# Decoder layer: five shared score banks, one pool for weights and transposed weights, block transposes in every duo

## Chip, cores and metric

The kernel runs on one core of a Trainium2 chip. The metric is device time in microseconds (us). Beside the runs that give the time there is one profiled execution; all lines of a profile come from it.

## The reference

One decoder layer on x of shape (4 batches, 1024 rows, 256 columns), all in float32. Three blocks follow one another, each on a layer norm of x and each added to x:

```
x = x + attn(layernorm(x))        # 16 heads of 64, 4 key/value heads, softmax over 1024 keys
x = x + cross_attn(layernorm(x))  # 16 heads of 16, 64 context rows
x = x + ffn(layernorm(x))         # routes each row to one of 64 tiles, gathers that tile's spline and direction
```

The first block is most of the work: for each batch and head `scores = q @ k.T` (1024 x 1024), `probs = softmax(scores)`, `out = probs @ v`.

## The kernel before

**Tiles and steps.** The queries of a batch are cut into 8 query tiles of 128 rows. A query tile has 16 heads. They are taken two at a time, and such a pair is a step: head z=0 lies on partitions 0 to 63 and head z=1 on partitions 64 to 127 of the query and key tiles. Two steps make a duo (`duo`, L566), four duos a query tile. In all there are 4 x 8 x 4 = 128 duos and 256 steps.

**One step.** TensorE writes the scores of two heads, 128 queries x 1024 keys each, into two PSUM tiles `s` of two banks each (`scores`, L589 to L598: four matmuls of 128x512, key half by key half). VectorE finds each row's maximum (`largest`, L606). ScalarE takes the exponential from PSUM into the SBUF tile `prob` and sums the rows on the way (`exponential`, L612). There are two such `s` tiles in the pool, so a step fills the pool, and the next step's matmuls write into the tiles that the exponentials are reading.

**Transposing.** The product with the values needs the weights with the keys on the partitions. Three of four duos (`by_array` false, L453) get there in two moves: VectorE transposes every 32x32 block in place (`turn`, L621, one instruction for a head), and then SyncE issues 16 DMAs of 128 KB (`carry`, L648) that carry blocks of 32 partitions from `prob` to their place in `probT`. Each fourth duo goes through TensorE: 32 transposes by the identity into the small PSUM tiles (`flips`, L631) and 8 ScalarE copies of 128x512 into `probT` (`evict`, L635).

**Values and output.** `values` (L671) multiplies `probT` with the values into the PSUM tile `av`, which has a bank of its own (`ps_o`), and ScalarE copies it to `heads` (L686). Once per query tile (`project`, L691) the row sums are inverted, turned (`rsT`), written to DRAM and spread back over the partitions (`rb`, L717 and L707, on SyncE's queue), GpSimd divides (`divide`, L710), and TensorE projects (`out_rows`, L728).

**PSUM.** Two `s` tiles of two banks, one bank for `av`, and three banks `p1` which every other matmul shares (`psum1`, L241): eight banks.

**What sets the order.** The order on every queue is planned while the program is built. Each piece of work is a `Task` with an engine, an assumed cost in us and a key (its due step). `Flow.order` (L120) plays the queues: it picks the task that could start first, urgent ones (scores, maxima, exponentials) ahead on a tie, and it holds a task that isn't urgent back if an urgent one will be ready within that task's cost (`soon`, L140 and L153). Tiles come in a number of places by tag (L228); a `Task` that takes a tile waits for a free place. The real tile pool hands its buffers out in turn. Each engine then executes its queue in the order that was written.

Of the kernel before, what the change touches and what calls it, by code (L numbers as in the profile page):

```python
# [17 lines left out]
P = 128  # L18
# [38 lines left out]
class Buf:  # L57


    def __init__(self, tag=None, make=None, whole=None):  # L60
        self.tag, self.make, self.whole = tag, make, whole or self
        self.writers, self.readers, self.parts = [], [], {}
        self.uses, self.first, self.left, self.last, self.t = set(), None, 0, 0.0, None

# [13 lines left out]
class Flow:  # L78
# [7 lines left out]
    AHEAD, SLACK = 16, 0.4  # L86
    LAG = {"PE": 0.3, "DVE": 0.2, "ACT": 0.25, "POOL": 0.25}
# [5 lines left out]
    def add(self, engine, cost, key, emit, reads=(), writes=(), lag=None, holds=(), lead=False, urgent=False):  # L93
# [4 lines left out]
        for b in writes:  # L98
            t.need.update(b.readers)
        t.need.discard(t)  # L100
# [19 lines left out]
    def order(self):  # L120
        free = {tag: [0.0] * n for tag, n in self.places.items()}
# [14 lines left out]
        while todo:  # L136
            best = None
            for engine, some in could.items():
                pick = None
                soon = min((t.ready for t in some if t.urgent), default=inf)  # L140
                for t in some:
# [4 lines left out]
                    for b in t.takes:  # L146
# [4 lines left out]
                        start = max(start, free[b.tag][k])  # L151
                    else:
                        if not t.urgent and start < soon < start + t.cost - self.SLACK:  # L153
                            start = soon
# [10 lines left out]
            for b in t.takes:  # L165
                free[b.tag].pop(0)
                if b.tag in self.lines:
                    self.lines[b.tag].remove(b)
# [8 lines left out]
            for b in t.bufs:  # L177
                b.left -= 1
                b.last = max(b.last, t.end)
                if not b.left:  # L180
                    insort(free[b.tag], b.last + 0.2)
            yield t

    def emit(self):
        for t in self.order():
            for b in t.takes:
                b.t = b.make()
# [5 lines left out]
def decoder(  # L193
# [26 lines left out]
    ps_s = ctx.enter_context(tc.tile_pool(name="ps_s", bufs=2, space=PSUM))  # L220
    ps_1 = ctx.enter_context(tc.tile_pool(name="ps_1", bufs=3, space=PSUM))
    ps_o = ctx.enter_context(tc.tile_pool(name="ps_o", bufs=1, space=PSUM))
# [5 lines left out]
            s=2, p1=3, o=1, x=3, xn1=2, xT=1, kT0=1, kT1=1, vn=4, qT=12, prob=2, probT=2, sums=3, nmax=4,  # L228
# [8 lines left out]
    def buf(tag, pool, *shape, bufs=None, name=None):  # L237
        bufs = flow.places[tag] if bufs is None else bufs
        return Buf(tag, lambda: pool.tile([P, *shape], F32, tag=tag, name=name or tag, bufs=bufs))

    def psum1(name):  # L241

        return Buf("p1", lambda: ps_1.tile([P, 512], F32, tag="p1", name=name))
# [159 lines left out]
    def layernorm(key, name, src, dst, w, reads, writes):  # L403

        st = Buf("ln", lambda: (
            small.tile([P, w, 6], F32, tag="bnst", name=f"{name}_st", bufs=2),
            small.tile([P, w, 2], F32, tag="bnmv", name=f"{name}_mv", bufs=2),
            small.tile([P, w], F32, tag="bnrs", name=f"{name}_rs", bufs=2),
# [20 lines left out]
        add("DVE", 0.6 * w, key, stats, reads, [st], holds=writes)  # L429
        add("POOL", 1.0, key, rsqrt, [st], [st])  # L430
        add("ACT", 0.45 * w, key, apply, [st, *reads], writes)

    def transposed(key, name, src, dst, k, reads, write):
# [12 lines left out]
        add("PE", 0.55, key, flips, reads, [pt], holds=[write])  # L446
# [6 lines left out]
    halves = (slice(0, HD), slice(HD, P))  # L453
    xs, xTs, kTs, vns, qTs, sums, heads = {}, {}, {}, {}, {}, {}, {}

    def by_array(d):

        return d % 4 == 3
# [27 lines left out]
    def keys(b, j, key):  # L486

        kT = kTs[b, j] = buf(f"kT{j}", big, S, name=f"kT_{b}_{j}")
        for g in range(2):
# [15 lines left out]
            add("PE", 1.75, key, project, [wk_, xTs[b].part(2 * g), xTs[b].part(2 * g + 1)], [pk], holds=[kT])  # L505
            add("ACT", 0.7, key, evict, [pk, colv_], [kT])

    def value_rows(b, g, key):
# [24 lines left out]
        add("PE", 1.75, key, project, [wv_, xTs[b].part(g)], [pv], holds=[vn])  # L533
        add("DVE", 0.69, key, evict, [pv, rowv_], [vn])

    def queries(b, w, c, key):
# [16 lines left out]
        add("PE", 1.8, key, project, [wq_, xTs[b].part(w)], [pq], holds=[qTs[b, w, c], qTs[b, w, c + 1]])  # L553
# [12 lines left out]
    def duo(b, d):  # L566
# [7 lines left out]
        prob = Buf("prob", lambda: work.tile([P, 4 * S], F32, tag="prob", name=f"prob_{b}_{d}"))  # L574
        probT = Buf("probT", lambda: work.tile([P, 4 * S], F32, tag="probT", name=f"probT_{b}_{d}"))
# [7 lines left out]
        for i in range(2):  # L583
# [3 lines left out]
            ps = [Buf("s", lambda z=z: ps_s.tile([P, S], F32, tag="s", name=f"s_{b}_{d}_{i}_{z}")) for z in range(2)]  # L587

            def scores(ps=ps, q=q, kT=kT):  # L589
                for g in range(2):  # L590
                    for z, r in enumerate(halves):
                        mm(  # L592
                            ps[z].t[:, 512 * g : 512 * (g + 1)],
# [6 lines left out]
            add("PE", 1.95, n - 3, scores, [q, kT], ps, holds=[prob, ss], lead=True)  # L600
            for z in range(2):
                k = z * QC + c
                nmax = buf("nmax", small, 1, name=f"nmax_{b}_{d}_{i}_{z}")

                def largest(z=z, nmax=nmax, ps=ps):
                    nc.vector.tensor_reduce(nmax.t, ps[z].t, AX.X, ALU.max, negate=True)  # L606

                def exponential(z=z, i=i, k=k, nmax=nmax, ps=ps):
                    src = ps[z].t
# [6 lines left out]
                add("DVE", 1.22, n - 3, largest, [ps[z]], [nmax], urgent=True)  # L616
                add("ACT", 1.33, n - 3, exponential, [ps[z], nmax], [prob.part((z, i)), ss.part(k)], urgent=True)
                if not by_array(d):
# [4 lines left out]
                    add("DVE", 1.25, n - 1, turn, [prob.part((z, i))], [prob.part((z, i))])  # L623
                else:
                    for g in range(2):
# [11 lines left out]
                        add("PE", 0.54, n - 1, flips, [prob.part((z, i))], [pt], holds=[probT])  # L637
                        add("ACT", 0.6, n - 1, evict, [pt], [probT.part((z, g))])

        if not by_array(d):  # L640


            for k in range(4):
                for qb in range(4):
                    r = (qb + k) % 4

                    def carry(qb=qb, r=r):
# [6 lines left out]
                        "SP", 0.6, at, carry, [prob.part((z, i)) for z in range(2) for i in range(2)],  # L654
# [4 lines left out]
        av = Buf("o", lambda: ps_o.tile([P, 2 * P], F32, tag="o", name=f"av_{b}_{d}"))  # L659
        jp = e // 2  # L660
        for part in range(2):
            def values(part=part):
                for kc in range(4 * part, 4 * part + 4):
                    for z, r in enumerate(halves):
# [3 lines left out]
                        else:  # L668
# [3 lines left out]
                            av.t[r, :],  # L672
# [7 lines left out]
                "PE", 1.9, at + 1, values,  # L680
# [4 lines left out]
        def evict():  # L685
            nc.scalar.copy(hd.t.rearrange("p c q -> p (c q)"), av.t)  # L686

        add("ACT", 0.45, at + 1, evict, [av], [hd])


    def project(b, qt):  # L691
# [4 lines left out]
        rT = Buf("rsT", lambda: small.tile([H, P], F32, tag="rsT", name=f"rsT_{b}_{qt}", bufs=1))  # L696
        rD = Buf("rsD", lambda: dram.tile([2, QC, P], F32, tag="rsD", name=f"rsD_{b}_{qt}"))
# [21 lines left out]
        for z, r in enumerate(halves):  # L719
            add("SP", 0.5, at - 4, lambda z=z, r=r: spread(z, r), [rD], [rb.part(z)], lag=2.5)  # L720
        for e in range(QC // 2):
            add("POOL", 0.6, at - 1, lambda e=e: divide(e), [rb.part(0), rb.part(1), hT[e]], [hT[e]])
        xb = x_part(b, qt)
        po, t = psum1(f"po_{b}_{qt}"), buf("res", work, D, name=f"res_{b}_{qt}")
        for part in range(2):
# [4 lines left out]
            add("PE", 1.75, at, out_rows, hT[2 * part : 2 * part + 2] + [wo_] + [po] * part, [po], holds=[t])  # L730
# [66 lines left out]
    def cross_attention(b, t0, at):  # L797
# [27 lines left out]
        add("PE", 1.8, at + 1, project_q, [xT, xwq_], [pq], holds=[qT])  # L825
# [3 lines left out]
        for k in range(TX):  # L829
# [15 lines left out]
            add("PE", 1.1, now, scores, [qT, kblk], ps, holds=[sc])  # L845
            for z in range(2):
# [9 lines left out]
                add("DVE", 0.75, now, masked, [ps[z], mneg_], [sc])  # L856
# [30 lines left out]
            add("POOL", 1.6, now + 1, add_up, [sc], [half], holds=[rs])  # L887
# [34 lines left out]
            add("PE", 0.9, now + 3, values, [pT.part(0), pT.part(1), vblk], [av], holds=[oT])  # L922
# [18 lines left out]
            add("PE", 0.9, now + 4, project_o, [oT, xwo_], [po], holds=[r])  # L941
# [4 lines left out]
    def calibrated(at, name, score, w, reads):  # L946
# [3 lines left out]
        def new(tag, *shape):  # L950
            return small.tile([P, *shape], F32, tag=tag, name=f"{name}_{tag}", bufs=1)
# [351 lines left out]
```

## Time and profile before

| | |
|---|---|
| median of 3 runs | 1978.22 us (1977.18 to 1980.28) |
| profiled execution | 1978.13 us, of which the span from first to last instruction is 1976.4 us |
| mean granted TensorE clock | 0.939 |
| busy in the span | TensorE 1737.7, VectorE 1400.9, ScalarE 1062.5, GpSimd 554.1 us |
| DMA | 243.05 MB; SyncE's queue takes 49.6% of 16 engines' span |
| first and last score matmul group start at | 36.8 and 1866.0 us |

Reading: the span splits into a head (36.8 us until the first scores), 255 intervals between steps (1829.2 us, 7.17 us each) and a tail (110.4 us from the start of the last scores). A line of a profile names the source line, the engine, the operation, what is written and read, the count, the busy time in us, the mean ns of one, and the idle time of the engine just before it with what ended that. A float32 matmul shows as two records.

### The profile page before, as it was taken

To read this page: it belongs to the slowest core of one execution; us is meant where nothing else is said; L and a number is where in the kernel's file an instruction comes from. 1 tells how busy PE (TensorE), PEld (TensorE's weight loads), DVE (VectorE), ACT (ScalarE), POOL (GpSimd) and SP (SyncE) were. 2 spreads that over 40 slices of the span, in tenths; PEclk is the share of its full clock that TensorE was granted. 3 is DMA by queue.
4 is the path that set the end of the run, shared out by engine and by line. 5 is a ranking of instruction groups with operands and counts; after the bars stand their busy time and mean duration, and the time that the engine had idled before them with its cause. 6 is when DMAs were issued, how large, how long until landed. Compare 5 with 4: busy or idle time off the path is not lost.

```text
span 1976.4 us, 28894 instructions
## 1 busy us (share of the span) xinstructions
PE 1737.7 (88%) x10180; PEld 1025.7 (52%) x10180; DVE 1400.9 (71%) x2036; ACT 1062.5 (54%) x1977; POOL 554.1 (28%) x872
## 2 busy tenths in 40 slices
PE   6898989889998998989999898988999899997842
PEld 4455555555654555555655454555555455554521
DVE  4667777886778766787677676787677876778632
ACT  3445556656564655655565555655565455555511
POOL 1001213152122512225031522316122350304352
PEclk8889999999998999999999898999999899999965
DMA  3566455455655455566454456545555645445500
GB/s 131 128 139 150 115 140 122 115 146 125 138 129 136 106 137 124 121 152 150 102 134 107 123 136 139 139 116 126 136 116 116 157 118 129 105 111 130 139 23 12
DMA packets 95455, 243.05 MB, mean 123 GB/s; under 512 B 28368, under 2 KB 39376, under 8 KB 95312
## 3 DMA queue, kind: packets, MB, share of 16 engines
q1 hardware_dynamic: 91504, 229.39, 49.6%
q0 software_dynamic: 2704, 9.46, 1.7%
q10 hardware_dynamic: 1104, 2.37, 0.3%
q8 instruction: 81, 1.33, 0.3%
q14 instruction: 62, 0.51, 0.1%
HBM read 35.32 MB, written 4.46 MB: 20 GB/s over the span
## 4 chain that ended last, share of the span: by engine, by line
PE 64%; DVE 16%; ACT 6%; POOL 5%; DMA 3%; SPq 3%; issue 3%; POOLq 0%; DVEq 0%; ACTq 0%
PE s L592 22%; PE av L671 18%; DVE nmax L606 6%; PE pq L545 5%; PE po L728 4%; PE ptp L631 4%; DVE prob L621 3%; SPq L648 3%; ACT prob L612 3%; PE pk L494 1%; PE pv L517 1%; DMA par<-in_table,tile 1%; PE pxt L898 1%; PE xs L837 1%; PE pxq L814 1%
## 5 line engine op out<-in xcount | busy, mean ns | idle before, releaser
L606 DVE TENSOR_REDUCE nmax<-s 128x1 f32<-128x1024 f32 x512 | 601.9, 1216 | 342.7 <-PE s L592 341.4
L612 ACT ACTIVATE prob<-s,nmax 128x1024 f32<-128x1024 f32 x512 | 568.8, 1114 | 407.3 <-DVE nmax L606 388.7
L592 PE MATMUL s<-kT,qT 64*128 64x512 f32 x2048 | 584.4, 639 | 35.0 <-ACT prob L612 34.6
L671 PE MATMUL av<-probT,vn 128*64 128x256 f32 x4096 | 499.4, 396 | 29.5 <-DMA probT<-prob 26.0
L621 DVE STREAM_TRANSPOSE prob<-prob 128x1024 f32<-128x1024 f32 x384 | 458.6, 1223 | 37.7 <-ACT prob L612 26.8
L671 PEld LDWEIGHTS av<-probT,vn 128*64 128x64 f32 x4096 | 298.2, 142 | 252.3 <-issue 111.7
L592 PEld LDWEIGHTS s<-kT,qT 64*128 64x128 f32 x2048 | 212.9, 192 | 266.5 <-issue 163.6
L710 POOL TENSOR_TENSOR heads<-heads,rb 128x256 f32<-128x256 f32 x128 | 90.0, 729 | 607.6 <-DMA rb<-rsD 503.7
L635 ACT COPY probT<-ptp 128x512 f32<-128x512 f32 x256 | 137.8, 590 | 74.3 <-PE ptp L631 72.5
L631 PE MATMUL ptp<-ident,prob 128*128 128x128 f32 x1024 | 141.1, 281 | 34.0 <-ACT prob L612 30.4
L631 PEld LDWEIGHTS ptp<-ident,prob 128*128 128x128 f32 x1024 | 112.8, 143 | 82.4 <-issue 37.6
L545 PE MATMUL pq<-ln_T,wq 128*128 128x256 f32 x512 | 127.6, 394 | 12.3 <-DVE xsc L849 12.3
L863 POOL TENSOR_TENSOR xsc<-xsc,xmx 128x1024 f32<-128x1024 f32 x32 | 61.2, 1914 | 248.2 <-DVE xmx L860 136.7
L728 PE MATMUL po<-wo,heads 128*128 128x256 f32 x512 | 119.2, 383 | 1.6 <-POOL heads L710 1.6
L545 PEld LDWEIGHTS pq<-ln_T,wq 128*128 128x128 f32 x512 | 95.3, 194 | 47.9 <-issue 29.2
L728 PEld LDWEIGHTS po<-wo,heads 128*128 128x128 f32 x512 | 95.5, 190 | 29.8 <-POOL heads L710 9.2
L612 ACT ACTIVATION_READ_ACCUMULATOR prob<-s,nmax 128x1 f32 x512 | 101.0, 197 | 0.0
L427 ACT ACTIVATE ln_n<-x,ln_mv,ln_rs 128x256 f32<-128x256 f32 x64 | 36.6, 596 | 107.1 <-POOL ln_mv L422 107.1
L686 ACT COPY heads<-av 128x256 f32<-128x256 f32 x128 | 47.6, 372 | 76.3 <-PE av L671 73.9
L556 ACT ACTIVATE qT<-pq,bqs,qscale 128x256 f32<-128x256 f32 x128 | 65.6, 564 | 35.6 <-PE pq L545 35.5
L419 POOL TENSOR_SCALAR ln_rs<-ln_mv 128x1 f32<-128x1 f32 (+1 forms) x96 | 21.4, 222 | 213.2 <-DVE ln_mv L415 200.7
L441 PE MATMUL ln_pt<-ident,ln_n 128*128 128x128 f32 x192 | 37.2, 312 | 44.9 <-ACT ln_n L427 42.4
(166 smaller groups left out, 1498.1 us busy)
## 6 DMA issues: line engine op xcount, KB each, us to landing
probT<-prob SPq DMA_DIRECT2D x1536, 128.0 KB, 2.3
rb<-rsD SPq DMA_DIRECT2D x64, 256.0 KB, 3.9
ln_n<-in_x SPq DMA_DIRECT2D x16, 256.0 KB, 3.1
x<-in_x SPq DMA_DIRECT2D x8, 512.0 KB, 4.9
out<-ln_n POOLq DMA_DIRECT2D x7, 512.0 KB, 4.9
wq<-in_w_qT ACTq DMA_DIRECT2D x1, 1024.0 KB, 8.0
wo<-in_w_oT SPq DMA_DIRECT2D x1, 1024.0 KB, 12.6
rowv<-in_rows ACTq DMA_DIRECT2D x1, 774.0 KB, 10.6
```

What stands on the lines that cost most here:

```text
L545: mm(pq.t[:, 2 * P * k : 2 * P * (k + 1)], lhsT=wq[:, dc, (c + k) * P : (c + k + 1) * P], rhs=xTs[b].t[:, dc, 2 * P * w : 2 * P * (w + 1)] ...
L556: nc.scalar.activation(qTs[b, w, c + k].t, pq.t[:, 2 * P * k : 2 * P * (k + 1)], AF.Identity, bias=bqs[:, c + k : c + k + 1], scale=qscale,)
L592: mm(ps[z].t[:, 512 * g : 512 * (g + 1)], lhsT=q.t[r, (qt % 2) * P : (qt % 2 + 1) * P], rhs=kT.t[r, 512 * g : 512 * (g + 1)], start=True, ...
L606: nc.vector.tensor_reduce(nmax.t, ps[z].t, AX.X, ALU.max, negate=True)
L612: nc.scalar.activation(weights(prob.t, z, i), src, AF.Exp, bias=nmax.t, accum_out=ss.t[:, k : k + 1])
L621: nc.vector.transpose(t, t)
L631: flip(pt.t[:, j * P : (j + 1) * P], weights(prob.t, z, i)[:, kc * P : (kc + 1) * P], ident)
L635: nc.scalar.copy(to[:, z, 4 * g : 4 * g + 4, i, :], pt.t.rearrange("p (c q) -> p c q", q=P))
L671: mm(av.t[r, :], lhsT=vns[b, kc // 2].t[:, kc % 2, j * HD : (j + 1) * HD], rhs=rhs, start=(kc == 0), stop=(kc == NT - 1),)
L710: nc.gpsimd.tensor_tensor(hT[e].t, hT[e].t, rb.t[:, 2 * e : 2 * e + 2, :], ALU.mult)
L728: mm(po.t[:, :D], lhsT=hT[c // 2].t[:, c % 2], rhs=wo[:, c, :], start=(c == 0), stop=(c == QC - 1))
L863: nc.gpsimd.tensor_tensor(sc.t, sc.t, mx.t.unsqueeze(2).to_broadcast([P, XH, SK]), ALU.subtract)
```

## The change

Five things change together.

- **Score banks.** The two `s` tiles and the bank of `av` become one PSUM tile of five banks. A step's heads take their banks by a rule of three (`ways`), so that a step has three of its four banks in common with the one before, and the scores of a step are two tasks (`part`), each of two matmuls.
- **av** moves into the three shared `p1` banks.
- **prob and probT** take their tiles from one pool of four places instead of two pools of two.
- **All duos** transpose by blocks: `by_array` returns False, so `flips` and its `evict` are issued for no duo, and every duo has four `turn` and 16 `carry`.
- **The planner**: fixed places (a tile gets the very place that the plan gave it, one buffer for each place), new costs and lags, and no holding back for urgent tasks.

```diff
-    AHEAD, SLACK = 16, 0.4
-    LAG = {"PE": 0.3, "DVE": 0.2, "ACT": 0.25, "POOL": 0.25}
+    AHEAD = 16
+    LAG = {"PE": 0.15, "DVE": 0.1, "ACT": 0.1, "POOL": 0.15}
...
+        for b in over:
+            t.need.update(b.readers)
+            b.readers, b.writers = [], [t]
...
-                soon = min((t.ready for t in some if t.urgent), default=inf)
...
-                        if not t.urgent and start < soon < start + t.cost - self.SLACK:
-                            start = soon
...
-                free[b.tag].pop(0)
+                b.place = free[b.tag].pop(0)[1]
...
-                b.t = b.make()
+                b.t = b.make(b.place)
...
-    ps_s = ctx.enter_context(tc.tile_pool(name="ps_s", bufs=2, space=PSUM))
+    ps_s = ctx.enter_context(tc.tile_pool(name="ps_s", bufs=1, space=PSUM))
     ps_1 = ctx.enter_context(tc.tile_pool(name="ps_1", bufs=3, space=PSUM))
-    ps_o = ctx.enter_context(tc.tile_pool(name="ps_o", bufs=1, space=PSUM))
...
-            s=2, p1=3, o=1, x=3, xn1=2, xT=1, kT0=1, kT1=1, vn=4, qT=12, prob=2, probT=2, sums=3, nmax=4,
+            p1=3, x=3, xn1=2, xT=1, kT0=1, kT1=1, vn=4, qT=12, prob=4, sums=3, nmax=4,
...
+    score_banks = ps_s.tile([P, 5, 512], F32, name="score_banks")
+    banks = [Buf() for _ in range(5)]
...
     def by_array(d):
 
-        return d % 4 == 3
+        return False
...
+            ways = (((0, 0), (2, 0)), ((3, 1), (0, 0)), ((1, 1), (3, 0)))[int(n) % 3]
+            ps = [score_banks[:, way[0] : way[0] + 2, :].rearrange("p g k -> p (g k)") for way in ways]
+            for part in range(2):
+                to = [way[0] + (part ^ way[1]) for way in ways]
+
+                def scores(part=part, ways=ways, to=to, q=q, kT=kT):
                     for z, r in enumerate(halves):
+                        g = part ^ ways[z][1]
                         mm(
-                            ps[z].t[:, 512 * g : 512 * (g + 1)],
+                            score_banks[:, to[z], :],
...
-            add("PE", 1.95, n - 3, scores, [q, kT], ps, holds=[prob, ss], lead=True)
+                add(
+                    "PE", 0.97, n - 3, scores, [q, kT], over=[banks[k] for k in to], holds=[prob, ss], lead=True
+                )
...
-        av = Buf("o", lambda: ps_o.tile([P, 2 * P], F32, tag="o", name=f"av_{b}_{d}"))
+        av = psum1(f"av_{b}_{d}")
```

The rule of three written out, with the bank of (key half 0, key half 1) of each head and the banks that the first and the second part write:

```
step mod 3   head 0   head 1   part 0   part 1
0            0, 1     2, 3     0, 2     1, 3
1            3, 4     0, 1     4, 0     3, 1
2            1, 2     3, 4     2, 3     1, 4
```

Of the planner's costs, scores go from 1.95 to 2 x 0.97, the maximum from 1.22 to 1.17, the exponential from 1.33 to 1.14, a block transpose from 1.25 to 1.19, a carry from 0.60 to 0.68, values from 1.90 to 1.87 a half, a query projection from 1.80 to 2.06, and some twenty others by similar amounts. Fixed places apply to all tags: a pool with `bufs=n` becomes n pools of one buffer.

## The prediction

> **What bounds the kernel now.** I read first the page's busy shares and its chain of work that ended last.
>
> ```profile
> PE 1737.7 (88%) x10180; PEld 1025.7 (52%) x10180; DVE 1400.9 (71%) x2036; ACT 1062.5 (54%) x1977; POOL 554.1 (28%) x872
> ...
> PE 64%; DVE 16%; ACT 6%; POOL 5%; DMA 3%; SPq 3%; issue 3%; POOLq 0%; DVEq 0%; ACTq 0%
> ```
>
> TensorE is busy 88% of the span and holds 64% of the chain; but 36% of the chain is elsewhere, so it isn't the only limit. Then the groups of instructions that the change touches:
>
> ```profile
> L606 DVE TENSOR_REDUCE nmax<-s 128x1 f32<-128x1024 f32 x512 | 601.9, 1216 | 342.7 <-PE s L592 341.4
> L592 PE MATMUL s<-kT,qT 64*128 64x512 f32 x2048 | 584.4, 639 | 35.0 <-ACT prob L612 34.6
> ...
> L621 DVE STREAM_TRANSPOSE prob<-prob 128x1024 f32<-128x1024 f32 x384 | 458.6, 1223 | 37.7 <-ACT prob L612 26.8
> ...
> L635 ACT COPY probT<-ptp 128x512 f32<-128x512 f32 x256 | 137.8, 590 | 74.3 <-PE ptp L631 72.5
> L631 PE MATMUL ptp<-ident,prob 128*128 128x128 f32 x1024 | 141.1, 281 | 34.0 <-ACT prob L612 30.4
> ```
>
> VectorE waits 341 us for scores before its maxima, and TensorE's scores wait for exponentials: a loop from step to step. The timeline shows the loop free of waits, and once caught:
>
> ```profile
> 709.23 3.08 PE L592 MATMUL s<-kT,qT 64*128 64x512 f32 x8 [0.45 <-ACT prob L612]
> ...
> 1016.96 1.99 PE L592 MATMUL s<-kT,qT 64*128 64x512 f32 x8
> ...
> 1018.98 2.35 DVE L606 TENSOR_REDUCE nmax<-s 128x1 f32<-128x1024 f32 x2 [0.66 <-PE s L592]
> ...
> 1020.23 1.11 ACT L612 ACTIVATE prob<-s,nmax 128x1024 f32<-128x1024 f32 x1 [0.24 <-DVE nmax L606]
> ...
> 1024.25 1.99 PE L592 MATMUL s<-kT,qT 64*128 64x512 f32 x8
> ```
>
> Scores take 1.99 us; the maxima start when they end; the first exponential starts 3.27 us after the scores did; the second ends 2.2 later. At 709.23 the first matmul could go when one exponential was through, and the group took 3.08 because the rest waited for the other. Last, SyncE's own waits and what one carry takes:
>
> ```profile
> SPq L648 <- DVE prob L621: 386.2, 84, 11.1
> ```
> ```profile
> probT<-prob SPq DMA_DIRECT2D x1536, 128.0 KB, 2.3
> ```
>
> SyncE mostly waits for the block transposes, in 84 of 96 duos: it has room.
>
> **What the Trainium skill says.** "VectorE: DVE Perf Modes", The three transpose paths: VectorE transposes only within 32x32 blocks, TensorE the whole, but into PSUM. The trace agrees: the first needs 16 carries, the second ScalarE copies of 590 ns. "PSUM — Partial Sum Buffer", The four PSUM rules: a matmul's output is at most one of eight banks; here a 128x512 score half is one, so five banks, not six, are what is left beside three shared ones. "TensorE: Matmul & The Clock Gate", Architectural detail: VectorE and ScalarE take their queues strictly in order. So a maximum waits behind any transpose queued before it. Same page, HAM oscillation: idle stretches of over about 3.4 us bring TensorE's clock down. The trace agrees: after 3.26 us of waiting at 1082.2 a score group took 4.91 us instead of 1.99.
>
> **The change, part by part**, against the profiled execution (1978.13 us, span 1976.4, so 1.7 around it; the median is 1978.22, the same).
>
> *TensorE transposes go.* TensorE loses 141.1 us, ScalarE 137.8 us. On TensorE this lies on the path wherever TensorE is the limit.
>
> *128 more block transposes* (32 duos of 4) at 458.6/384 = 1.19 us: VectorE gains 153 us, to 1554. TensorE falls to 1597, and to about 1520 if the score groups' stalls go as well (584.4 less 256 x 1.99 is 75 us). So the two become equal.
>
> *512 more carries on SyncE.* One takes 0.63 us (14 in 8.84 us at 699.85), 2048 take 1290 us. A duo needs 16 x 0.63 = 10.1 us, and a query tile 40.3 plus 1.4 for `rsD` and `rb` plus up to 2.6 waiting on `rsD`: 44.3. Hidden as long as a query tile takes more. `values` of a duo stands two duos behind its scores in the new order, about 26 us; transposes end some 6 us after the scores, and carries and landing (2.3) make 18.4: 7 us to spare. Behind the carries on this queue stand the loads of x, `rsD` and `rb`; in the chain 16 carries (738.5 to 748.6) already precede a load that ScalarE waits for. Each fourth duo now puts 10.1 us ahead of them. The next such load is due many steps ahead, so I cost it at nothing; without that cover it is 10 us for each of 24 loads at worst, 240, in the range only for a small part (up to 40).
>
> *Banks.* A step shortens its loop: from the end of scores 0.1 + maximum 1.18 + 0.1 + two exponentials 2.22 + 0.1 + scores 1.99 = 5.7 us before. By the rule of three, one step in three needs only the first exponential (4.6), the other two need the second only for their second half, 1.0 us long (4.7). So 1.0 less. What the loop really costs is read where no engine is full: query tiles whose TensorE work sums to 48.2 and VectorE work to 40.5 take 54.6 to 56.4 us, 6.9 a step; 1.2 is work that stands in the way. I take 5.9, and 6.0 since VectorE has four more transposes in eight steps; nothing holds them back for an urgent maximum now (at most one, 1.2 us, per step).
>
> *av in the shared banks.* It holds one of three places 3.67 + 0.37 us and lags in each duo, a third of the time; behind the TensorE work that waits for a place stand the next scores. Shortage of places costs TensorE 12.3 us today (query projections waiting for L849). Bound: 0 to 25 us. *Fixed places* end waits on a place that the plan hadn't meant: -12 to 0. I take 0 for both together.
>
> *One pool of four.* No bytes more; a duo's first exponential can take whichever tile is free. ScalarE waits 17.8 us on that today; 0 to -18, taken as 0, since all duos now hold both tiles for the length of the carries.
>
> *The tail.* The last duo was flipped by TensorE: its values ended 14.7 us after its scores began (1866.0 to 1880.7). Now: scores 2.0, maximum and two exponentials 3.5, last transpose 1.5, carries 10.1, landing 2.3, values 3.7: 23.1. That is 8.5 more with nothing behind to cover it.
>
> *The sum.* I counted the instructions of each engine between one query tile's scores and the next, in the order each kernel is built in, times the durations above (VectorE's less 3%, for neighbours overlap). In a batch of the middle, us:
>
> ```
> query tile        0     1     2     3     4     5     6     7
> before: TensorE 55.1  58.2  48.2  49.6  48.2  53.9  49.8  59.3
>         VectorE 39.0  42.8  52.7  37.9  39.3  40.7  52.9  40.1
> after:  TensorE 54.1  51.2  44.4  47.9  41.2  52.1  45.2  51.3
>         VectorE 41.5  47.4  56.9  45.4  43.4  45.4  56.9  45.4
> ```
>
> Before, tiles full of TensorE work took about 1% more than that work (0, 5, 7), tiles full of VectorE work about 5 us more. After: tiles 0, 1, 5, 7: 208.7 x 1.01 = 210.8; tiles 2 and 6: 113.8 + 10 = 123.8; tiles 3 and 4 at the loop's floor, 2 x 8 x 6.0 = 96. Sum 430.6. Before, a batch took 457.3 (1829.2/4). So 26.7 less, four times: 107. 1978.1 - 107 + 8.5 = 1880.
>
> **Rivals.**
>
> *Smooth overlap* (about 1800): the banks let a heavy tile run into a light one, and the plan with costs nearer to the trace wastes less. Then the mean counts: 418.5 a batch without overheads, 156 less, and 20 to 30 more by overlap across tiles. For it: TensorE reached 97 to 98% in some stretches of 100 us. Against: the two engines are now both nearly full, with a step of slack between them.
>
> *The carries bind* (about 1910): if DMA engines, busy 50% now and a third more to move in less time, make a carry 0.80 us instead of 0.63, a duo needs 12.8 plus 0.9 for its part of `rsD` and `rb`: 13.7 x 128 = 1754, with head 37 and tail 119: 1910. For it: every carry waits until the one eight before it has landed, and the longest landing was 7.2 us. Against: the median is 2.3.
>
> *VectorE as the new bound, slower* (about 2015). VectorE's work between first and last scores rises from 1350 to 1503, 5.89 us a step, against 7.17 that a step takes now. It idles 1.88 a step there now, 1.28 of it waiting for scores. Point of decision: if it still idles over 1.28 a step, the change loses. At 1.4, 7.29 x 255 + 37 + 119 + 2 = 2015. The mechanism is its strict queue: transposes without holding back delay the maximum, this delays exponential and scores, and VectorE then waits for scores. For it: 341 us of such waits. Against: the loop has 1.0 us less in it.
>
> *It doesn't do as it says:* if the single tile of five banks were guarded as one, each score would wait for all reads. The built order shows score halves with waits of their own, so I give this nothing apart from the slower case.
>
> **How the numbers follow.** Forecast 1880 (1835 to 1925): 0.54. Smooth: 0.15. Carries bind: 0.15. Slower: 0.13. Within 0.2%, about what a measurement can tell from no change: 0.03. Faster: 0.54 + 0.15 + 0.15 less 0.01 for their edges, 0.83; same 0.03; slower 0.14. The range reaches from the smooth case to past the carries, 1800 to 1965; it leaves out the slower case and half of the smooth one's lower side. The unknown costs (25, -12, -18) lie within it.
>
> **What would show it.** The page after should have TensorE near 1590 us busy and VectorE near 1554, both at about 84%; score groups of 1.99 us where they were caught at 3; VectorE's wait for scores well under 341 us; carries still 0.63 us apart and landing in under 3; a tail about 8 us longer. I am wrong if VectorE waits for scores as before, if SyncE's queue runs without a gap, or if `values` waits for carries by over 50 us.

## The result, and the profile after

The changed kernel takes 2270.46 us (median of 4 runs, 2267.72 to 2277.89), the kernel before, run beside it on the same chip, 1979.25 us (1977.18 to 1981.07). The ratio is 1.148, with a 95% interval of 1.145 to 1.151: slower by 15%, where 1880 us was forecast. The profiled execution has a span of 2269.5 us, 293 us more than before, at a mean granted TensorE clock of 0.887 instead of 0.939.

The page's busy times of the changed kernel, and its costliest groups that answer to those shown of before:

```profile
PE 1685.3 (74%) x9156; PEld 910.0 (40%) x9156; DVE 1565.8 (69%) x2164; ACT 926.3 (41%) x1721; POOL 557.3 (25%) x872
...
L621 ACT ACTIVATE prob<-score_banks,nmax 128x1024 f32<-128x1024 f32 x512 | 566.6, 1110 | 969.3 <-DVE nmax L615 602.6
L597 PE MATMUL score_banks<-kT,qT 64*128 64x512 f32 x2048 | 611.8, 712 | 439.7 <-ACT prob L621 439.5
L615 DVE TENSOR_REDUCE nmax<-score_banks 128x1 f32<-128x1024 f32 x512 | 601.9, 1217 | 338.9 <-PE score_banks L597 338.7
L630 DVE STREAM_TRANSPOSE prob<-prob 128x1024 f32<-128x1024 f32 x512 | 615.7, 1225 | 229.1 <-ACT prob L621 224.4
L680 PE MATMUL av<-probT,vn 128*64 128x256 f32 x4096 | 499.2, 397 | 11.6 <-DMA probT<-prob 11.6
```

For comparison, the exponentials in the kernel before:

```profile
L612 ACT ACTIVATE prob<-s,nmax 128x1024 f32<-128x1024 f32 x512 | 568.8, 1114 | 407.3 <-DVE nmax L606 388.7
```

No engine is full any more: TensorE falls from 88% to 74%. The instructions of VectorE and ScalarE cost what they did (a maximum 1217 ns, an exponential 1110, a transpose 1225); a score record on TensorE takes 712 ns on average, 639 before. What grew most is the idle time in front of them: TensorE waits 439.5 us for exponentials before its scores, where it waited 34.6; the exponentials wait 602.6 us for maxima, where they waited 388.7; the transposes wait 224.4 us for exponentials, where it was 26.8. VectorE's wait for scores is unchanged, 338.7 after 341.4. The three engines of the step wait for one another in a ring. (The chain of work that ended last can be followed back through only a tenth of this trace, so the waits are read instead.)

The timeline of the changed kernel shows two kinds of step; some rows are left out:

```profile
1033.05 2.36 DVE L615 TENSOR_REDUCE nmax<-score_banks 128x1 f32<-128x1024 f32 x2 [2.95 <-PE score_banks L597]
...
1035.50 1.11 ACT L621 ACTIVATE prob<-score_banks,nmax 128x1024 f32<-128x1024 f32 x1 [3.69 <-DVE nmax L615]
...
1043.39 1.11 ACT L621 ACTIVATE prob<-score_banks,nmax 128x1024 f32<-128x1024 f32 x1 [1.23 <-DMA probT<-prob]
...
1044.65 1.13 PE L597 MATMUL score_banks<-kT,qT 64*128 64x512 f32 x4 [1.47 <-ACT prob L621]
...
1045.83 1.11 ACT L621 ACTIVATE prob<-score_banks,nmax 128x1024 f32<-128x1024 f32 x1 [0.74 <-PE score_banks L597]
...
1047.09 2.08 PE L597 MATMUL score_banks<-kT,qT 64*128 64x512 f32 x4 [1.30 <-ACT prob L621]
...
1049.28 2.35 DVE L615 TENSOR_REDUCE nmax<-score_banks 128x1 f32<-128x1024 f32 x2 [2.19 <-PE score_banks L597]
...
1051.73 1.11 ACT L621 ACTIVATE prob<-score_banks,nmax 128x1024 f32<-128x1024 f32 x1 [4.43 <-DVE nmax L615]
```

First: the maxima of both heads begin at 1033.05, and the first exponential, which needs only the first of them, starts at 1035.50, 2.45 us later, when both are through. In the kernel before it started 1.25 us after them (1018.98 to 1020.23, in the lines that the prediction shows). This holds for every step: in the changed kernel's trace none of the 256 first exponentials starts before the second maximum has ended, in that of before 251 do. Second: at 1043.39 an exponential, at 1044.65 the first half of the next scores, at 1045.83 the second exponential, at 1047.09 the second half. Each begins only when the one ahead has ended, and the exponential at 1045.83 is held up by scores of the next step (0.74 us, put down to L597), which it doesn't need.

The waits that are written into the two programs say why. Each row names an instruction and, of those on VectorE and ScalarE that read the tile, the last one whose end it waits for; the number behind @ is where in the tile it starts, 512 to a bank:

```
changed kernel
  exponential, head 0 <- score_banks@512     waits for: maximum of head 1 <- score_banks@1536
  scores -> score_banks@0 (first half)       waits for: exponential of head 1 <- score_banks@1536
kernel before
  exponential, head 0 <- s (head 0's tile)   waits for: maximum of head 0 <- s (head 0's tile)
  exponential, head 1 <- s (head 1's tile)   waits for: maximum of head 1 <- s (head 1's tile)
```

In the changed kernel the exponential of banks 1 and 2 waits for a maximum that reads banks 3 and 4. The program keeps the accesses of different engines to one tile apart in the order in which they are written, reads from reads too, and does so for the whole tile of five banks. **The theory** is thus the rival to which the prediction gave nothing: the tile is guarded as one. The loop of a step is then scores 1.99, both maxima 2.35, both exponentials 2.22 and 0.3 between them, 6.9 us, where it was 5.7. The chip doesn't ask for it. The Trainium skill ("PSUM — Partial Sum Buffer", Terms) has two engines collide on one and the same bank and quadrant (32 partitions), two reads included; in the trace of before ScalarE read one `s` tile at 1020.23 while VectorE was reading the other until 1021.33, which agrees, since those are other banks. **The rivals**: that the planner, which no longer holds back for urgent work, is at fault; that the carries are (VectorE and SyncE have a third more of transposes and carries); or that `av` crowds the shared banks.

### The profile page after: what moved, and what is told of

The parts are those of the page before. It is cut to its first block, busy times and chain, and to the rows that moved or that the text cites. A ratio compares the mean times of both kernels' runs of the same rounds, so it can differ in the third digit from the quotient of the medians.

```text
span 2269.5 us, 28413 instructions
## 1 busy us (share of the span) xinstructions
PE 1685.3 (74%) x9156; PEld 910.0 (40%) x9156; DVE 1565.8 (69%) x2164; ACT 926.3 (41%) x1721; POOL 557.3 (25%) x872
## 5 line engine op out<-in xcount | busy, mean ns | idle before, releaser
L621 ACT ACTIVATE prob<-score_banks,nmax 128x1024 f32<-128x1024 f32 x512 | 566.6, 1110 | 969.3 <-DVE nmax L615 602.6
L597 PE MATMUL score_banks<-kT,qT 64*128 64x512 f32 x2048 | 611.8, 712 | 439.7 <-ACT prob L621 439.5
L615 DVE TENSOR_REDUCE nmax<-score_banks 128x1 f32<-128x1024 f32 x512 | 601.9, 1217 | 338.9 <-PE score_banks L597 338.7
L630 DVE STREAM_TRANSPOSE prob<-prob 128x1024 f32<-128x1024 f32 x512 | 615.7, 1225 | 229.1 <-ACT prob L621 224.4
L680 PE MATMUL av<-probT,vn 128*64 128x256 f32 x4096 | 499.2, 397 | 11.6 <-DMA probT<-prob 11.6
L597 PEld LDWEIGHTS score_banks<-kT,qT 64*128 64x128 f32 x2048 | 192.7, 208 | 689.3 <-ACT prob L621 545.4
L621 ACT ACTIVATION_READ_ACCUMULATOR prob<-score_banks,nmax 128x1 f32 x512 | 100.0, 195 | 0.0
L894 POOL TENSOR_TENSOR xsc<-xsc,xrs 128x1024 f32<-128x1024 f32 x32 | 60.8, 1900 | 65.3 <-DVE xrs L891 65.3
L418 POOL TENSOR_TENSOR ln_rs<-ln_rs,minus_half 128x1 f32<-128x1 f32 (+1 forms) x96 | 59.6, 621 | 8.0
L947 POOL TENSOR_TENSOR x<-x,xres 128x256 f32<-128x256 f32 x32 | 23.2, 724 | 153.7 <-DVE xres L944 153.7
L858 DVE TENSOR_TENSOR xsc<-xs,mneg 128x256 f32<-128x256 f32 x128 | 45.0, 414 | 19.1 <-PE xs L846 18.2
```

The source lines that it names most:

```text
L418: nc.gpsimd.tensor_tensor(rs, rs, minus_half.to_broadcast([P, w]), ALU.pow)
L597: mm(score_banks[:, to[z], :], lhsT=q.t[r, (qt % 2) * P : (qt % 2 + 1) * P], rhs=kT.t[r, 512 * g : 512 * (g + 1)], start=True, stop=True,)
L615: nc.vector.tensor_reduce(nmax.t, ps[z], AX.X, ALU.max, negate=True)
L621: nc.scalar.activation(weights(prob.t, z, i), src, AF.Exp, bias=nmax.t, accum_out=ss.t[:, k : k + 1])
L630: nc.vector.transpose(t, t)
L680: mm(av.t[r, : 2 * P], lhsT=vns[b, kc // 2].t[:, kc % 2, j * HD : (j + 1) * HD], rhs=rhs, start=(kc == 0), stop=(kc == NT - 1),)
```

## Experiments

Every kernel ran beside the kernel before, whose median was between 1975.8 and 1980.1 us.

### One guard, and nothing else

The kernel before, with its two score tiles cut from one tile. Instructions, order and banks are the same; only the waits differ.

```diff
-    ps_s = ctx.enter_context(tc.tile_pool(name="ps_s", bufs=2, space=PSUM))
+    ps_s = ctx.enter_context(tc.tile_pool(name="ps_s", bufs=1, space=PSUM))
...
+    score_banks = ps_s.tile([P, 2, S], F32, name="score_banks")
...
-            ps = [Buf("s", lambda z=z: ps_s.tile([P, S], F32, tag="s", name=f"s_{b}_{d}_{i}_{z}")) for z in range(2)]
+            ps = [Buf("s", lambda z=z: score_banks[:, z, :]) for z in range(2)]
```

> The kernel before with one thing changed: its two score tiles are cut out of one PSUM tile of four banks; same instructions, same banks, same order. Theory (one tile is guarded as one, so each head's exponential waits for both maxima, 1.17 us more, and scores wait for both exponentials): the loop of a step grows from about 5.7 to 6.9 us, at most 307 us in 256 steps, part of it covered by TensorE work: 2120 to 2280 us. Rivals (VectorE's queue with 128 more transposes and no holding back; the carries): nothing of theirs is in it, 1978 us within 0.5%.

2125.33 us, a ratio of 1.076 (1.071 to 1.081): 149 us for the waits alone. The waits of this kernel:

```profile
ACT prob L613 <- DVE nmax L607: 408.9, 181, 8.9
DVE nmax L607 <- PE score_banks L593: 349.9, 200, 10.9
...
PE score_banks L593 <- ACT prob L613: 175.8, 116, 4.9
...
DVE prob L622 <- ACT prob L613: 126.8, 116, 1.4
```

It is the signature of the changed kernel at half its size: scores wait 175.8 us for exponentials (34.6 before), transposes 126.8 (26.8 before), and the wait for scores hardly moves (349.9). A guard that is wider than the data is shown as a cause; it isn't all of the 293 us.

### The changed kernel without the one tile

Two separate score tiles of two banks again, and `av` in its own bank. Planner, fixed places, pool of four and block transposes in all duos stay.

```diff
-    score_banks = ps_s.tile([P, 5, 512], F32, name="score_banks")
...
-            ways = (((0, 0), (2, 0)), ((3, 1), (0, 0)), ((1, 1), (3, 0)))[int(n) % 3]
...
+            ps = [
+                Buf("s", lambda k, z=z: ps_s.tile([P, S], F32, tag=f"s_{k}", name=f"s_{b}_{d}_{i}_{z}", bufs=1))
+                for z in range(2)
+            ]
...
-        av = psum1(f"av_{b}_{d}")
+        av = Buf("o", lambda k: ps_o.tile([P, 512], F32, tag="o", name=f"av_{b}_{d}"))
```

> The changed kernel with the banks undone: two score tiles of two banks, av in a bank of its own; all duos by blocks, the pool of four, fixed places and the new planner stay. Theory of the shared guard: 1860 to 1980 us, VectorE's wait for scores well down and ScalarE's wait for maxima back near 390 us. Rivals (VectorE's queue order, or the carries, make it slow): stays above 2150 us.

1957.99 us, 0.990 (0.987 to 0.994). All of the loss is gone, and so planner, pool and block transposes together aren't its cause. But it is only 1% faster than before, and far from 1880. VectorE's wait for scores came down as expected (186.0 us), while ScalarE's wait for maxima, expected near 390 us, is 510.9. Its page and its chain:

```profile
PE 1682.2 (86%) x9156; PEld 937.6 (48%) x9156; DVE 1559.6 (80%) x2164; ACT 933.7 (48%) x1721; POOL 556.1 (28%) x872
...
PE 40%; SPq 22%; DVE 18%; DMA 10%; ACT 4%; issue 4%; POOL 2%; DVEq 0%; POOLq 0%; ACTq 0%
```

SyncE's queue holds 22% of the chain and DMA 10%, against 3% each before. SyncE's own waits, and its queue over some 36 us of a query tile:

```profile
SPq L652 <- DMA probT<-prob: 199.4, 233, 3.9
...
SPq L652 <- DVE prob L625: 58.8, 33, 5.1
```
```profile
899.41 36.11 SPq L652 DMA_DIRECT2D probT<-prob  x43
```

SyncE waits hardly for transposes any more (58.8 us; it was 386.2) but for earlier carries to land (199.4 us). 43 carries in a row take 36.11 us, 0.84 each, and the prediction's 0.63 came from a train of 14. They are part of a longer train, and beside a short one of the same kernel the length shows:

```profile
738.52 10.25 SPq L652 DMA_DIRECT2D probT<-prob  x16
...
883.36 52.16 SPq L652 DMA_DIRECT2D probT<-prob  x64
```

16 carries take 0.64 us each, 64 take 0.82. So here the rival "the carries bind", priced at 0.80, is at work.

### Block transposes in all duos, alone and left out

The kernel just shown with every fourth duo through TensorE again; and the kernel before with block transposes in all duos, nothing else changed.

```diff
-        return False
+        return d % 4 == 3
```

> As the one before, and each fourth duo goes through TensorE again: what is left of the change is the planner (costs, lags, no holding back), fixed places and the pool of four. Theory of the shared guard: 1930 to 1990 us, near the kernel before. Rival (no holding back delays maxima): above 2050 us.

1927.88 us, 0.976 (0.973 to 0.978): the fastest of all. Its page and its chain:

```profile
PE 1735.3 (90%) x10180; PEld 1011.8 (52%) x10180; DVE 1398.2 (72%) x2036; ACT 1053.4 (54%) x1977; POOL 555.7 (29%) x872
...
PE 52%; DVE 20%; ACT 7%; POOL 6%; SPq 6%; issue 4%; DMA 4%; ACTq 0%; DVEq 0%; POOLq 0%
```

TensorE does the same work as before (1735.3 us) in 42 us less of span, and SyncE is back at 6% of the chain.

```diff
-        return d % 4 == 3
+        return False
```

> The kernel before with all duos transposed by blocks and nothing else changed: 141 us of TensorE work less, 153 us of VectorE work and 512 carries more. Theory of the shared guard: the carries and transposes are not the trouble, 1900 to 2040 us. Rivals (VectorE as the bound, or the carries): above 2150 us, with TensorE's values waiting for carries by over 100 us in the carries' case.

2060.05 us, 1.041 (1.036 to 1.046): above the theory's range (1900 to 2040), though below the rivals' 2150, so the block transposes and their carries do cost something. The same edit costs 30 us with the new planner and pool and about 82 without. Where TensorE waits in this kernel:

```profile
PE s L592 <- ACT prob L612: 117.9, 67, 4.1
...
ACT prob L612 <- DMA probT<-prob: 80.8, 25, 6.3
PE av L671 <- DMA probT<-prob: 63.8, 25, 5.4
```

`values` waits 63.8 us for carries (26.0 before) and the exponentials 80.8 us for carries to set their tile free. TensorE's 141 us of transposes went, but its page total fell by 10.7 us only (1737.7 to 1727.0): its other groups took longer, the scores 651.8 us in place of 584.4 and the values 532.9 in place of 499.4.

### The same guard in the new order

The kernel with two tiles (1957.99) with both cut from one tile of four banks: the first experiment repeated in the order of the new planner.

```diff
+    score_banks = ps_s.tile([P, 2, S], F32, name="score_banks")
...
-                Buf("s", lambda k, z=z: ps_s.tile([P, S], F32, tag=f"s_{k}", name=f"s_{b}_{d}_{i}_{z}", bufs=1))
+                Buf("s", lambda k: score_banks[:, k, :])
```

> The changed kernel with two score tiles of two banks and av in its own bank, but the two cut out of one tile of four banks: the shared guard alone, beside the run that had them as separate tiles (1958 us). Theory that the guard is nearly all of the loss: 2150 to 2270 us. Rival, that the other half of the 312 us is the plan: the planner counts on early scores and on halves that the guard forbids, and the halves hold exponentials up; then the guard alone adds about what it added to the kernel before, 150 us: 2070 to 2130 us.

2160.91 us, 1.094 (1.090 to 1.098): 203 us more than with two tiles. Its waits:

```profile
ACT prob L617 <- DVE nmax L611: 513.6, 156, 7.4
...
PE score_banks L597 <- ACT prob L617: 344.1, 175, 11.0
...
DVE prob L626 <- ACT prob L617: 213.9, 196, 2.9
```

The guard is worth two thirds of the whole loss. 110 us are left between this kernel and the changed one, and three things that differ: `av`, the rule of three, the halves.

### What the other 110 us are

First `av` moved into the three shared banks, with the score tile as just now.

```diff
-        av = Buf("o", lambda k: ps_o.tile([P, 512], F32, tag="o", name=f"av_{b}_{d}"))
+        av = psum1(f"av_{b}_{d}")
```

> Two score tiles cut from one tile of four banks, and av in the three shared banks as in the changed kernel. av in shared banks cost 28 us where it was tried with a fourth shared bank (1928 to 1956). With three, I expect 2161 plus 20 to 50: about 2195, the loop of the scores leaving some of it covered. If av in the shared banks is most of the changed kernel's remaining 110 us, this gives 2250 or more; if the loop covers it all, 2160.

2156.15 us, 1.091 (1.088 to 1.094). `av` costs nothing here: the expectation of about 2195 was wrong, the loop of the scores covers it.

Then the changed kernel itself, its five banks and the rule of three kept, with a step's four score matmuls as one task.

```diff
-            for part in range(2):
-                to = [way[0] + (part ^ way[1]) for way in ways]
...
+            def scores(ways=ways, q=q, kT=kT):
+                for part in range(2):
...
-                    "PE", 0.97, n - 3, scores, [q, kT], over=[banks[k] for k in to], holds=[prob, ss], lead=True
+            add("PE", 1.94, n - 3, scores, [q, kT], over=[banks[k] for k in own], holds=[prob, ss], lead=True)
```

> The changed kernel with the rule of three and its five banks, but a step's four score matmuls written as one task instead of two halves. One tile guarded as one costs about 203 us (two tiles cut from one: 2161 against 1958); the changed kernel is another 110 us slower. If that rest is the halves, which the order puts between the two exponentials so that the second exponential waits for the half behind the first, this gives about 2160 to 2190. If it is that the plan counts on three banks in common, so that everything behind the scores stands at the wrong place, halves or not, it stays at 2240 to 2280.

2156.8 us, 1.091 (1.088 to 1.093): 114 us less than the changed kernel, from the halves alone. The rule of three and the plan that counts on it cost nothing. Its waits:

```profile
ACT prob L618 <- DVE nmax L612: 500.4, 157, 6.4
...
PE score_banks L595 <- ACT prob L618: 359.0, 173, 10.9
...
DVE nmax L612 <- PE score_banks L595: 220.4, 180, 4.7
```

VectorE waits 220.4 us for scores, 118 less than in the changed kernel. In the order of the changed kernel the first half of the next scores stands between a step's two exponentials in 48 of 256 steps; here in none. The halves were to start the scores earlier. But with one guard the second exponential waits for a half that stands ahead of it. In the changed kernel's trace, the time from the start of a step's scores to the start of the next is 10.08 us where the scores came in more than one piece (56 steps) and 7.76 where they came in one (199); with whole scores it is 7.84 on average. 56 x 2.3 is 130, and not all of these 56 are due to the order, so the 114 are covered. Of these 2.3 us a step, the lines of the timeline account for some 0.5. Exponential, half, exponential, half are 1.11 + 1.13 + 1.11 + 1.13 = 4.5 us in a row (with the usual 1.13 for the slow half at 1047.09), plus gaps of 0.35; two exponentials and whole scores are 2.2 + 2.0 = 4.2, plus one gap of 0.15. What makes up the rest was not tried.

### The shared banks, the carries' queue and the pool

Three score tiles of two banks each, `av` in the shared banks, and only two of these. It gives TensorE a place to write ahead, with separate guards.

```diff
-    score_banks = ps_s.tile([P, 5, 512], F32, name="score_banks")
...
-            p1=3, x=3, xn1=2, xT=1, kT0=1, kT1=1, vn=4, qT=12, prob=4, sums=3, nmax=4,
+            s=3, p1=2, x=3, xn1=2, xT=1, kT0=1, kT1=1, vn=4, qT=12, prob=4, sums=3, nmax=4,
```

> The changed kernel with three separate score tiles of two banks, av in the shared banks, of which two are left: half a step of real room ahead, no shared guard. Forecast's own loop argument (a shorter loop is worth most of 107 us): 1850 to 1920 us. Rival, that the carries bind once all duos use them (43 carries took 36.1 us, 0.84 each, with no gap): no gain over two separate tiles, 1940 to 2000 us.

1990.37 us, 1.007 (1.004 to 1.010), in the rival's range and not in the forecast's. Against two tiles (1958) the third tile's gain, if any, is less than the price of `av` in the shared banks and of one shared bank fewer; this run doesn't part them. A wait that tells it:

```profile
ACT heads L689 <- PE av L674: 199.9, 78, 17.8
```

With two tiles it was 105.7 us: `values` come later, and one copy to `heads` waits 17.8 us for them.

Then the two-tile kernel with a quarter of the carries issued by ScalarE.

```diff
-                        nc.sync.dma_start(
+                        (nc.scalar if k == 3 else nc.sync).dma_start(
```

> Two separate score tiles, all duos by blocks, and a quarter of the carries (4 of 16 in a duo) issued by ScalarE instead of SyncE. If SyncE's queue of carries binds: 12 x 0.8 us in a duo instead of 16, 1860 to 1930 us against 1958. If it is the DMA engines, or VectorE, that bind: 1940 us or more, and more still as ScalarE gives 2 us per duo to the issuing.

1982.17 us, 1.002 (1.000 to 1.004), 24 more than with SyncE alone. SyncE's waits:

```profile
SPq L652 <- DMA probT<-prob: 417.0, 331, 5.1
SPq L652 <- DVE prob L625: 150.6, 52, 7.5
```

With fewer carries of its own SyncE waits longer for earlier ones to land, 417.0 us in place of 199.4. So issuing isn't what limits the carries; their landing is the likelier limit. That ScalarE's time went into the loss as well isn't excluded.

Then the fastest kernel (1928) with `av` in the shared banks, of which there are four, and no bank of its own.

```diff
-            s=2, p1=3, o=1, x=3, xn1=2, xT=1, kT0=1, kT1=1, vn=4, qT=12, prob=4, sums=3, nmax=4,
+            s=2, p1=4, x=3, xn1=2, xT=1, kT0=1, kT1=1, vn=4, qT=12, prob=4, sums=3, nmax=4,
```

> Two separate score tiles, each fourth duo through TensorE, and av with four shared banks instead of a bank of its own. If av in the shared banks costs TensorE waits for places: slower than 1928 us. If four shared places are worth more than a bank of its own: 1900 to 1928 us.

1955.71 us, 0.989 (0.985 to 0.993): 28 us more, though there are as many banks. With no guard in the way a bank of its own for `av` is worth something.

Last the fastest kernel with two pools of two in place of one of four.

```diff
-            s=2, p1=3, o=1, x=3, xn1=2, xT=1, kT0=1, kT1=1, vn=4, qT=12, prob=4, sums=3, nmax=4,
+            s=2, p1=3, o=1, x=3, xn1=2, xT=1, kT0=1, kT1=1, vn=4, qT=12, prob=2, probT=2, sums=3, nmax=4,
```

> The fastest kernel so far (two score tiles, every fourth duo through TensorE, new planner, 1928) with two pools of two tiles again for weights and transposed weights instead of one of four. My sum gave the pool nothing: 1928 within 8 us. If the pool of four is what made that kernel faster than the one before, it goes back to 1945 to 1980; if each kind having its own two tiles is better, under 1920.

1959.01 us, 0.988 (0.983 to 0.993). The pool of four is worth about 31 us by the medians (24 by the two ratios; one of the four times here is 1940), and what is left, new planner and fixed places, about 18 (the interval leaves 13 to 35). One wait of it is shorter with four, that of the exponentials for carries out of their tile: 39.7 us here, 13.0 with the pool of four. The 26.7 us between them are most of the 31, if they count in full.

### Would a shorter loop have helped?

The fastest kernel with a step's scores as two tasks, one for each head. A head's scores then wait for its own exponential only: an early start of one exponential, which is what the five banks were to give, with separate tiles.

```diff
-            def scores(ps=ps, q=q, kT=kT):
-                for g in range(2):
-                    for z, r in enumerate(halves):
+            for z, r in enumerate(halves):
+                def scores(z=z, r=r, ps=ps, q=q, kT=kT):
+                    for g in range(2):
...
-            add("PE", 1.94, n - 3, scores, [q, kT], ps, holds=[prob, ss], lead=True)
+                add("PE", 0.97, n - 3, scores, [q, kT], [ps[z]], holds=[prob, ss], lead=True)
```

> The fastest kernel so far (two score tiles, every fourth duo through TensorE, 1928) with a step's scores as two tasks, one for each head, each waiting for its own head's exponential only. It gives the step's loop what the five banks were to give it, about one exponential (1.1 us) less, without a shared tile. If the loop is what limits, 1870 to 1910. If the two heads' matmuls run side by side only when they alternate on the two halves of the array's rows, the scores take up to twice 1.99 us: 512 more us of TensorE work at worst, at 90% busy, so 2000 to 2400. If neither matters, 1920 to 1936.

2108.33 us, 1.068 (1.064 to 1.071). TensorE's rows in the timeline of this kernel:

```profile
1009.84 1.99 PE L596 MATMUL s<-kT,qT 64*128 64x512 f32 x8
1011.76 1.95 PE L675 MATMUL av<-probT,vn 128*64 128x256 f32 x16
1014.43 1.98 PE L596 MATMUL s<-kT,qT 64*128 64x512 f32 x4 [0.72 <-ACT prob L616]
1016.34 1.95 PE L675 MATMUL av<-probT,vn 128*64 128x256 f32 x16
1018.22 1.98 PE L596 MATMUL s<-kT,qT 64*128 64x512 f32 x4
```

One head alone (4 records, two matmuls) takes 1.98 us, as long as both heads together (8 records) at 1009.84. So the two heads run side by side where their matmuls are neighbours, and the plan has now put half of `values` between them (1016.34). The scores' busy time goes from 600.6 to 732.0 us. The experiment thus says nothing on the loop: what it may win in waiting it pays in matmuls that no longer run side by side. Whether five banks with a guard each would give the prediction's 1.0 us stays open. It wasn't tried: one maximum and one exponential read two banks in one instruction, so with these instructions a bank can't be a tile of its own.

## Why the prediction was wrong

From one kernel to the next, each differing from the one above in what its row names (what a step costs depends on the order of the rows: one tile cost 149 us in the kernel before, 203 here):

| | us | step |
|---|---|---|
| before | 1976 to 1980 | |
| new planner, fixed places | 1959 | about -18 |
| pool of four | 1928 | about -31 |
| block transposes in all duos | 1958 | +30 |
| one tile for the scores | 2161 | +203 |
| `av` in the shared banks | 2156 | -5 |
| five banks, rule of three | 2157 | 0 |
| scores in halves | 2270 | +114 |

- **The step that failed** is the one named *Banks*: "So 1.0 less". It took a step's loop from 5.7 to 4.7 us on the assumption that an access waits only for accesses to the same banks. With one tile guarded as one the loop is 6.9 by the sum above (7.8 from step to step in the trace with whole scores), and with halves between exponentials further. Together +317 us. The prediction had the right mechanism among its rivals ("if the single tile of five banks were guarded as one") and dismissed it with "The built order shows score halves with waits of their own, so I give this nothing". That the halves had waits was true, and said nothing: what had to be read is whom each wait names. The first exponential's wait for the other head's maximum stood in the built program.
- **The point of decision for "slower"**, VectorE idle over 1.28 us a step, was well placed: from the first scores (37.2) to the last (2145.0) a step now takes 8.27 us, of which VectorE works 5.93 (the prediction counted 5.89) and idles 2.3. Of its three signs of being wrong one came: VectorE waits for scores as before. But the mechanism given for it, transposes ahead of a maximum in VectorE's strict queue, isn't what did it: with the same planner and two tiles the kernel takes 1958.
- **The carries.** "Carries bind" had 0.80 us a carry and 1910 us. Once the guard is out, the price is right (0.82 to 0.84 in the long train), and moving the transposes is a loss of 30 us; that kernel takes 1958, longer than this rival's 1910. The forecast's 0.63 was mis-sized: it came from a train of 14, and a query tile has 64. In the changed kernel itself the longer loop hides them: `values` waits 11.6 us for carries, the exponentials 60.8.
- **TensorE's busy time.** 1590 was forecast and 1685.3 came. The 141.1 us of transposes went, but other groups took longer (among them scores +27.4, output projection +13.9, query projection +7.2 us), at a granted clock of 0.887 in place of 0.939. The clock isn't all of it, since the kernel with two tiles has 1682.2 us at 0.924. The prediction itself cited the Trainium skill on this ("TensorE: Matmul & The Clock Gate", HAM oscillation: idle stretches bring the clock down) and didn't apply it to its own sum. The trace agrees: all 21 score matmul records that begin after more than 4 us of idle TensorE take over 900 ns, 1210 on average, where the shortest take 589. (The group at 1082.2 that the prediction reads for this ran at a granted clock of 0.50, but after 3.26 us, a little less than the page's figure, and some 0.9 of its 4.91 us, an estimate from what twice 1.99 leaves, is a wait for the second exponential, as at 709.23.)
- **VectorE's busy time**: 1554 forecast, 1565.8 measured. Right.
- **Pool of four**: 0 taken, bound 0 to -18; about -31. **Fixed places** with the new costs: bound -12 to 0; about -18. **`av`**: bound 0 to 25; nothing under the guard, 28 without. All three were near their bounds or past them, and none decides.
- **The tail**: +8.5 forecast, 14.1 measured (124.5 from the start of the last scores, against 110.4).
- **Readings of the sum** that were off, though they don't decide. In the trace of before, from score start to score start, the fifth query tile of a batch (number 4, 48.2 us of TensorE work) takes 55.6 us in the first batch and 59.4 to 59.9 in the others, 7.0 to 7.5 a step, where the prediction read 54.6 to 56.4; and the third (number 2), full of VectorE work, takes 64.7 to 67.0 in the last three, 12 to 14 more than the 52.7 counted, where 5 was allowed. So the floor and the overhead were set low. The slower case at 1.4 us sums to 2017, not 2015.

## What to carry to other kernels

Before a buffer is cut into parts that are to be used independently, read in the built program which instruction each wait names, for reads as well: a guard over the whole buffer turns independent reads into a chain, and this cost 149 us in one order and 203 in another with no instruction changed. Splitting a task in two for an earlier start puts the first half ahead of something else; ask what waits for it there. And take the price of a transfer from a train as long as the one that is planned, not from a short one.

## What the runs showed of the hardware

- Two score matmuls of one head (64 rows of the array) take 1.98 us, four of two heads on the two halves of the rows 1.99, if no other matmul stands between the heads. This agrees with the Trainium skill ("TensorEngine Tiling (Array Packing)", Theoretical Speedup: a contraction of 64 or less may gain up to twice). An order of matmuls that looks indifferent is worth up to that.
- Carries of 128 KB from SyncE, waits for earlier ones to land included: 0.63 us each in a train of 14, 0.64 in one of 16, 0.82 in one of 64, and a second queue to issue them made the kernel no faster (1982 against 1958 us).
- With TensorE busy 74% in place of 88%, its mean granted clock was 0.887 in place of 0.939, and a score record took 712 ns in place of 639. 383 of the 2048 score records took over 900 ns, against 97 before, among them all 21 that came after more than 4 us of idle TensorE. So long waits cost more than their own length.
